# Bilinear products from twelve turned copies, and a full complex transform per image, in a four-layer kernel on one core

## The chip, the cores and the metric

The kernel runs on one core of a Trainium2 chip. The metric is the device time of one execution in microseconds (us). Three executions of the kernel before gave 5891.43, 5906.5 and 5907.27 us; their median is 5906.5. The first of them is the one that the profiler recorded.

## The reference

Four images of 96 channels and 64 x 64 pixels (4096 pixels each, also called tokens) pass through four layers: a recurrent (Mamba) layer with a fusion and a batch norm, a bilinear layer, and two token layers. Only the last three matter here. In the bilinear layer every pixel has a channel vector p (96 values, after a group norm and a 3 x 3 mean), and each output channel is a quadratic form in it. In a token layer the pixels are normed, widened to 192 channels, taken through a Fourier transform over all 4096 tokens, changed frequency by frequency, and brought back; a feed-forward pass with 8-bit rounding follows.

```python
# layer 1
wm = weight * mask
t = jnp.einsum('nlc,ocd->nlod', p, wm)
y = jnp.einsum('nlod,nld->nlo', t, p) + bias
...
# layers 2 and 3, attention
h = jax.nn.relu(_bn(jnp.einsum('bnc,hc->bnh', x, w1), ...))
X = jnp.fft.fft(h, axis=1, norm='ortho')
xr = jax.nn.relu(X.real * rd - X.imag * idg + rb)
xi = jax.nn.relu(X.imag * rd + X.real * idg + ib)
y = jnp.fft.ifft(xr + 1j * xi, axis=1, norm='ortho').real
o = _bn(jnp.einsum('bnh,ch->bnc', y, w2), ...)
...
# layers 2 and 3, feed-forward
h = jax.nn.relu(_qlinear(x, W1, b1))
y = _qlinear(h, W2, b2)
```

The mask of the bilinear weights has a zero diagonal and keeps about one entry in ten, but the kernel treats all pairs of channels alike. Since a quadratic form is symmetric, the weights of (c, d) and (d, c) can be added, and each unordered pair needs one product: 96 x 97 / 2 = 4656 of them.

## The kernel before

One function per stage runs after the other. `_mamba` (to about 2977 us) and `_norms_and_pool` (line 437) are the same in both kernels. The last thing that the norms do is to write the pooled image twice, one copy under the other, to a DRAM buffer `p2[b]` of 192 rows (line 523), so that any turn of the channels is one run of rows.

`_bilinear` (line 526) first makes the weights: seven groups of seven rotations are loaded on SP's queue into staging tiles with two buffers each (lines 535 to 551), masked and summed on VectorE into `wk`. Then it goes through 4 images and 4 column blocks of `CW` = 1024 pixels. For each block it loads the 96 channels `p0`, and for each of 48 turns k = 1 to 48 the channels turned by k (`rot`, 384 KB each, eight buffers, line 565); VectorE multiplies the two into `z` (line 566; k = 0 is a square on ScalarE, line 562), and TensorE adds weights times `z` to `p_y` by two matmuls of N = 512 columns with 96 rows (line 568). So there are 49 products a block. After four blocks the image is turned to token order by TensorE and written to DRAM as `tok[b]` on SP's queue (line 583).

`_tokens` (line 586) begins with loads and small calculations for the parameters of both layers (lines 598 to 649), then loads all four images as two tiles of an image pair (lines 840 to 845). For each layer it runs `attention` for pair 0 and pair 1 and then `ffn` for both; `finish` writes both pairs at the end. An attention works on two images together:

- `stats` takes mean and variance with one `bn_stats` per token row on VectorE (line 665); `normed` applies them on GpSimd, four rows at a time (line 683).
- Each group of four rows is transposed on TensorE (`plt`, line 699), copied by ScalarE (`lnT`), multiplied by `w1` (`ph`, line 706, N = 192) and clamped on VectorE into `dst`.
- The transform of 4096 = 128 x 32 is done in two steps. The first, `pa` (line 714), takes 32 matmuls of N = 384 (192 channels of two images) against tables `k_fwd` that hold 64 cosines and 64 sines, half of the frequencies, since the input is real. Three 128 x 4096 transposes on VectorE (line 722) bring the result to channel order, and `px` (line 730) does the second step with 96 matmuls of N = 128, whose stationary operand is a strided slice of the transposed tile.
- ScalarE and VectorE apply the change by frequency (lines 739 to 756), with the two special frequencies apart (`ends`); `pv` (lines 761 to 765) multiplies by `w2`, so that the way back has 96 channels instead of 192.
- `pg` (lines 777 to 779) and `poo` (line 787) are the two steps back. `poo` takes 32 matmuls of N = 192 for both images, and VectorE adds the result to the tokens.

`ffn` (line 791) is a chain by groups of four rows: norm, rounding to 8 bits, transpose, three matmuls `pf1` with a copy and a clamp each, rounding (`hq`, one buffer), twelve small matmuls `pf2`, copy, two adds.

Inside the recurrent stage the order is written by hand (`manual_schedule`). Elsewhere a scheduler of the framework orders the instructions of each engine's queue, by the dependences and the buffers free; within a queue the order is then fixed.

Of the kernel before, what the change touches and what calls it, by code (L numbers as in the profile page):

```python
# [9 lines left out]
F32 = mybir.dt.float32  # L10
# [17 lines left out]
H = 192  # L28
# [4 lines left out]
NROT = C // 2 + 1  # L33
CW = 1024

_V_LNG, _V_LNB = 0, 2
_V_GPB, _V_FUSB, _V_BNG, _V_BNB, _V_L1B = 4, 5, 6, 7, 8
_NV = 9
# [487 lines left out]
def _bilinear(ctx, tc, io, w, f_all, p2, tok):  # L526


    nc = tc.nc
    wp = ctx.enter_context(tc.tile_pool(name="bw", bufs=1))  # L530
    stage = ctx.enter_context(tc.tile_pool(name="bst", bufs=2))
# [5 lines left out]
    NK = 7  # L537
    wk = wp.tile([C, NROT, C], F32, name="wk", tag="wk")
    for k0 in range(0, NROT, NK):
        part = []  # L540
        for n, (lo, hi) in (("1", (0, NROT)), ("2", (1, NROT - 1))):
            a, e = max(k0, lo), min(k0 + NK, hi)
            wt = stage.tile([C, NK, C], F32, name=f"wt{n}_{k0}", tag=f"wt{n}")
            mt = stage.tile([C, NK, C], F32, name=f"mt{n}_{k0}", tag=f"mt{n}")
            nc.sync.dma_start(wt[:, : e - a, :], io["bw" + n][:, a - lo : e - lo, :])
            nc.sync.dma_start(mt[:, : e - a, :], io["bm" + n][:, a - lo : e - lo, :])
            out = wk[:, a:e, :] if n == "1" else wt[:, : e - a, :]
            nc.vector.tensor_tensor(out, wt[:, : e - a, :], mt[:, : e - a, :], ALU.mult)
            part.append((a, e, wt))
        a, e, wt = part[1]  # L550
        nc.vector.tensor_tensor(wk[:, a:e, :], wk[:, a:e, :], wt[:, : e - a, :], ALU.add)

    for b in range(B):
        for q in range(L // CW):
            cols = slice(q * CW, (q + 1) * CW)
            p0 = work.tile([C, CW], F32, name=f"p0_{b}_{q}", tag="p0", bufs=2)
            nc.sync.dma_start(p0, p2[b][0:C, cols])
            p_y = ps.tile([C, CW], F32, name=f"py2_{b}_{q}", tag="py2")
            for k in range(NROT):
                z = work.tile([C, CW], F32, name=f"z_{b}_{q}_{k}", tag="z")  # L560
                if k == 0:
                    nc.scalar.activation(z, p0, AF.Square)  # L562
                else:
                    rot = work.tile([C, CW], F32, name=f"rot_{b}_{q}_{k}", tag="rot", bufs=8)
                    nc.sync.dma_start(rot, p2[b][k : k + C, cols])
                    nc.vector.tensor_tensor(z, p0, rot, ALU.mult)  # L566
                for n in range(CW // 512):
                    nc.tensor.matmul(  # L568
                        p_y[:, n * 512 : (n + 1) * 512],
                        wk[:, k, :],  # L570
                        z[:, n * 512 : (n + 1) * 512],
                        start=(k == 0),
                        stop=(k == NROT - 1),
                    )
# [11 lines left out]
def _tokens(ctx, tc, io, w, tok, out):  # L586

    nc = tc.nc
    wp = ctx.enter_context(tc.tile_pool(name="tw", bufs=1))
    ps_x = ctx.enter_context(tc.tile_pool(name="tpsx", bufs=3, space=PSUM))
    ps = ctx.enter_context(tc.tile_pool(name="tps", bufs=5, space=PSUM))
    ident = w["ident"]
    H2 = 2 * H
# [3 lines left out]
    mats = _load(nc, wp, io["k_mats"].rearrange("p (a m) -> p a m", a=4), [128, 4, 128], "mats")  # L600
    bd, bd0, ibd, ibd0 = (mats[:, i, :] for i in range(4))
    att = _load(nc, wp, io["att"], [128, 2 * 12], "att")
    neg = wp.tile([128, 2 * 12], F32, name="neg", tag="neg")
    nc.vector.tensor_scalar(neg, att, -1.0, None, ALU.mult)  # L604

    prm = []
    with tc.tile_pool(name="tset", bufs=1) as sp:
        for i in range(2):
            d = {}
            bn1 = sp.tile([C + 1, 4, H], F32, name=f"bn1_{i}", tag="ld1")  # L610
# [12 lines left out]
            for h in range(4):  # L623
                nc.vector.tensor_tensor(d["w2"][:, h], d["w2"][:, h], s2, ALU.mult)
# [29 lines left out]
    def large(name, shape):  # L654
        n = 1
        for s in shape:
            n *= s
# [346 lines left out]
```

## Time and profile before

| | |
|---|---|
| median of three executions | 5906.5 us |
| the profiled execution: its own time | 5891.43 us |
| its span in the trace | 5889.6 us |
| granted TensorE clock, mean | 0.898 |
| TensorE busy | 4825.0 us (82%) |
| VectorE busy | 4617.2 us (78%) |
| ScalarE busy | 2609.6 us (44%) |
| GpSimd busy | 3007.2 us (51%) |
| recurrent stage | 0 to about 2977 us |
| norms and pooling | to about 3144 us |
| bilinear stage: weights, then products | 3144 to 3178, to 4538 us |
| token stage: parameters and first loads | 4538 to 4603 us |
| four attentions of two images | 4603 to 4838, to 5048; 5245 to 5450, to 5660 us |
| feed-forward passes, two images twice | 5048 to 5245; 5660 to 5853 us |
| `finish` | 5853 to 5889.6 us |

The span runs from the first instruction to the last; an execution's own time lies a little above it. In the page's rows, `PE` is TensorE and `PEld` its loading of stationary operands. The tokens stage's times come from the first and last instruction on the tiles named above. A matmul on fp32 data leaves two records in the trace, so 1568 bilinear matmuls appear as 3136 records. The mean of a group of records is the time that the trace gives one record, and neighbours overlap; how long a matmul holds the engine is read from the distance between starts.

### The profile page before, as it was taken

Reading aid. Unit: us, or ns where it says so; the run is one execution under the profiler, and the core shown is the slowest. Engines: PE = TensorE matmul, PEld = TensorE weight load, DVE = VectorE, ACT = ScalarE, POOL = GpSimd, SP = SyncE. Lnnn points to the kernel's source line nnn. Section 1 sums busy time; section 2 is a strip of 40 time slices with the busy share of each in tenths; the row PEclk is TensorE's granted clock in tenths of the full one; section 3 lists DMA queues with packets and bytes.
Section 4 is the critical chain, followed back from the end, with each engine's and each line's share of the span. In section 5 each row is a group of like instructions: output and inputs, shape, how many; then the busy total and the mean of one; then the engine's idle time right before and its main releaser. Section 6 shows DMA issues by size and latency. Waiting matters only on the chain.

```text
span 5889.6 us, 47897 instructions
## 1 busy us (share of the span) xinstructions
PE 4825.0 (82%) x13508; PEld 2140.2 (36%) x13508; DVE 4617.2 (78%) x5787; ACT 2609.6 (44%) x5545; POOL 3007.2 (51%) x2129
## 2 busy tenths in 40 slices
PE   7888888888888898888714999999998577567765
PEld 2333333333333333333201333333333466346643
DVE  5999999999999999999995767767675475756564
ACT  5676676666766766666520000000000155335445
POOL 5999999999999999999910000000000211230211
PEclk9999999999999999999956999999999688668875
DMA  4453543534535445344347888888886200000001
GB/s 103 93 119 72 111 104 79 121 85 98 116 71 117 94 88 119 80 103 107 76 134 202 234 233 232 230 235 229 235 230 179 73 15 15 15 3 20 22 11 43
DMA packets 167379, 669.02 MB, mean 114 GB/s; under 512 B 28356, under 2 KB 31366, under 8 KB 132168
## 3 DMA queue, kind: packets, MB, share of 16 engines
q1 hardware_dynamic: 167112, 665.96, 45.2%
q8 instruction: 107, 1.75, 0.1%
q14 instruction: 160, 1.31, 0.1%
HBM read 630.20 MB, written 35.65 MB: 113 GB/s over the span
## 4 chain that ended last, share of the span: by engine, by line
PE 34%; DVE 7%; DMA 3%; ACT 3%; issue 2%; POOL 1%; SPq 1%; ACTq 0%; DVEq 0%; POOLq 0%
PE py L568 23%; PE ph L706 2%; PE px L730 2%; PE pf L819 1%; PE pv L761 1%; DVE hq L815 1%; PE pa L714 1%; ACT y L812 1%; DVE a L722 1%; DVE r L813 1%; PE pf L810 1%; PE pg L779 1%; DMA k_inv<-in_k_inv 1%; DMA k_fwd<-in_k_fwd 1%; PE pv L764 1%
## 5 line engine op out<-in xcount | busy, mean ns | idle before, releaser
L367 POOL TENSOR_TENSOR dbx<-du,bq 128x1024 f32<-128x1024 f32 x768 | 1804.5, 2355 | 3.3 <-DMA bq<-rows 3.2
L388 PE MATMUL py<-hc,ident 128*128 128x512 f32 x3072 | 1601.6, 627 | 134.5 <-DVE hc L377 110.0
L568 PE MATMUL py<-z,wk 96*96 96x512 f32 x3136 | 1350.6, 593 | 68.9 <-DMA rot<-p 68.9
L566 DVE TENSOR_TENSOR z<-p,rot 96x1024 f32<-96x1024 f32 x768 | 935.6, 1221 | 395.2 <-PE py L568 393.5
L374 DVE TENSOR_TENSOR_SCAN da<-da,hst,dbx 128x512 f32<-128x512 f32 x864 | 1099.4, 1272 | 1.2 <-POOL dbx L367 1.2
L361 ACT ACTIVATE da<-delta,aneg 128x512 f32<-128x512 f32 x1536 | 1058.7, 690 | 91.4 <-DVE hs L374 71.4
L388 PEld LDWEIGHTS py<-hc,ident 128*128 128x128 f32 x3072 | 555.8, 195 | 1095.2 <-issue 531.4
L377 POOL TENSOR_TENSOR hc<-hs,cq 128x512 f32<-128x512 f32 x672 | 854.1, 1271 | 185.9 <-DVE hs L374 99.0
L701 POOL MEMSET lnT<- 1x512 f32 x64 | 33.2, 520 | 1628.2 <-DVE neg L604 1564.4
L374 DVE TENSOR_TENSOR_SCAN hs<-da,hst,dbx 128x512 f32<-128x512 f32 x672 | 856.1, 1274 | 9.0 <-ACT da L361 9.0
L568 PEld LDWEIGHTS py<-z,wk 96*96 96x96 f32 x3136 | 511.3, 163 | 898.5 <-issue 829.5
L377 DVE TENSOR_TENSOR hc<-da,cq 128x512 f32<-128x512 f32 x864 | 597.8, 692 | 81.0 <-DMA cq<-rows 4.4
L562 ACT ACTIVATE z<-p 96x1024 f32<-96x1024 f32 x16 | 16.9, 1056 | 1292.5 <-PE py L568 1225.1
L381 ACT COPY hst<-da 128x1 f32<-128x1 f32 x864 | 136.3, 158 | 728.6 <-DVE hc L377 718.4
L683 POOL TENSOR_SCALAR x_f<-t,m_f,r_f 128x96 f32<-128x96 f32 x256 | 130.8, 524 | 512.6 <-DVE q L799 512.4
L224 PE MATMUL pc<-xs,taps 128*128 128x512 f32 x768 | 381.6, 594 | 0.0
L683 POOL TENSOR_SCALAR x_a<-t,m_a,r_a 128x96 f32<-128x96 f32 x256 | 107.8, 437 | 415.9 <-PE plt L699 352.0
L730 PE MATMUL px<-mats,a 128*128 128x128 f32 x768 | 184.2, 398 | 72.3 <-DVE a L722 69.9
L198 PE MATMUL pr<-r,picks 128*96 128x512 f32 x128 | 110.6, 965 | 151.6 <-DVE r L194 151.6
L224 PEld LDWEIGHTS pc<-xs,taps 128*128 128x128 f32 x768 | 145.7, 190 | 185.5 <-issue 175.3
L208 PE MATMUL pxz<-hn,in_w 96*64 96x512 f32 x768 | 212.0, 622 | 0.0
L730 PEld LDWEIGHTS px<-mats,a 128*128 128x128 f32 x768 | 174.1, 312 | 78.1 <-DVE a L722 74.7
(231 smaller groups left out, 5217.0 us busy)
## 6 DMA issues: line engine op xcount, KB each, us to landing
rot<-p SPq DMA_DIRECT2D x768, 384.0 KB, 4.3
bq<-rows SPq DMA_DIRECT2D x256, 512.0 KB, 6.8
cq<-rows SPq DMA_DIRECT2D x256, 512.0 KB, 10.2
p<-pt SPq DMA_DIRECT2D x8, 1536.0 KB, 12.6
k_fwd<-in_k_fwd SPq DMA_DIRECT2D x32, 256.0 KB, 2.8
k_inv<-in_k_inv SPq DMA_DIRECT2D x32, 256.0 KB, 2.7
x<-in_x SPq DMA_DIRECT2D x16, 384.0 KB, 9.1
fd<-f SPq DMA_DIRECT2D x32, 192.0 KB, 2.0
```

What stands on the lines that cost most here:

```text
L208: nc.tensor.matmul(q[h, :], in_w[:, l, 64 * kk : 64 * kk + 64], hn[b], start=True, stop=True)
L224: nc.tensor.matmul(p_c[k], taps[:, (l * 3 + k) * 4 + j, :], xs[k][:, j : j + TC], start=(j == 0), stop=(j == 3))
L361: nc.scalar.activation(da[u], st[n]["delta"][k], AF.Exp, scale=aneg[:, at : at + 1])
L367: nc.gpsimd.tensor_tensor(t, st[n]["du"][k].unsqueeze(1).to_broadcast([128, 2, TC]), b, ALU.mult)
L374: nc.vector.tensor_tensor_scan(hs[u], da[u], dbx[u], hst[:, at : at + 1], ALU.mult, ALU.add)
L377: (nc.gpsimd if on_pool(u) else nc.vector).tensor_tensor(hc[u], hs[u], c, ALU.mult)
L381: nc.scalar.copy(hst[:, at : at + 1], hs[u][:, TC - 1 : TC])
L388: nc.tensor.matmul(py[n, k], ident, hc.pop(u), start=(s == 0), stop=(s == 15))
L566: nc.vector.tensor_tensor(z, p0, rot, ALU.mult)
L568: nc.tensor.matmul(p_y[:, n * 512 : (n + 1) * 512], wk[:, k, :], z[:, n * 512 : (n + 1) * 512], start=(k == 0), stop=(k == NROT - 1),)
L683: nc.gpsimd.tensor_scalar(x[:, j, :], t[:, k, :], m[:, k : k + 1], r[:, k : k + 1], ALU.add, ALU.mult)
L730: nc.tensor.matmul(p_x[:, k, :], a2[:, 128 * m : 128 * m + 128, k0 + k], bd0 if k0 + k == 0 else bd, start=True, stop=True,)
```

## The change

In the bilinear stage the 49 products a block of 96 rows become 37. Twelve turned tiles of 128 rows (96 rows turned by one shift, and the first 32 rows of another shift below them, two DMAs each from `p2`) are loaded once a block, each kind with two buffers. The products are one square (96 rows, ScalarE) and 36 products of one of the first six tiles with one of the last six (128 rows, VectorE). The shifts are chosen so that each pair of channels occurs; where a pair occurs twice, the second weight is zero. The weights are correspondingly 128 x 37 x 96, loaded in ten groups of four products, with one staging buffer of each kind. Matmuls keep N = 512. In SP's new order, the loads of turned tiles 0 to 5 of the first block stand between the weight groups, those of tiles 6 to 11 after all of them; the store of `tok[b]` stands after the first turned loads of the next image, and the token stage's first loads (image 0, first parameters) stand ahead of the last such store.

In the token layers the transform of half of the frequencies for a pair of images becomes a full complex transform for one image at a time, so there are eight attentions instead of four:

- `layernorm` works on a whole image: two reductions, a subtraction and a multiplication of 128 x 3072 on VectorE and a square on ScalarE, in place of `stats` and `normed`; GpSimd has only the small fills left.
- `k_fwd` and `k_inv` hold all 128 cosines and 128 sines (512 KB a table of four rows, three buffers). `pa` becomes 64 matmuls of N = 192, the transposes four of 128 x 3072, `px` 128 matmuls of N = 256 with 96 channels of stationary operand, two accumulated into one result.
- The change by frequency is two ScalarE instructions (`cross`) and two VectorE instructions (`zz`) for each of 16 tiles, without special frequencies.
- `pv` becomes 128 matmuls of N = 96 with two copies for each pair of k, `pg` 24 of N = 512 in pairs, and `poo` for each of 32 rows one matmul with a single row (the shift of the second norm) and two with the tables, N = 96 each.
- Images are taken in pairs, one pair after the other: load two, both layers, `finish`, then the next two. The large tiles share four `slot` buffers of 24 KB a partition; `px` has two PSUM buffers of two banks and all else four.

`ffn` keeps its steps, on a whole-image norm, with two buffers for `hq` and a tile of its own (`o2`) for the first add. Constants and layouts change to match (`_layout`, `_constants`). The diff's core, with removed lines that the listing above shows left out:

```diff
-NROT = C // 2 + 1
 CW = 1024
...
+_TURNS = [(s, (32 * (i % 3) + 16 * (i // 3)) % C) for i, s in enumerate((0, 76, 60, 44, 32, 88))]
+_TURNS += [(s, 32 * (i % 3) + (2, 6)[i // 3]) for i, s in enumerate((25, 1, 73, 49, 24, 48))]
+_PAIRS = [(0, 0)] + [(i, j) for j in range(6, 12) for i in range(6)]
...
     wp = ctx.enter_context(tc.tile_pool(name="bw", bufs=1))
-    stage = ctx.enter_context(tc.tile_pool(name="bst", bufs=2))
+    stage = ctx.enter_context(tc.tile_pool(name="bst", bufs=1))
+    turned = ctx.enter_context(tc.tile_pool(name="bturn", bufs=2))
     work = ctx.enter_context(tc.tile_pool(name="bwork", bufs=3))
     ps = ctx.enter_context(tc.tile_pool(name="bps", bufs=2, space=PSUM))
...
+    NK = 4
+    NT = len(_PAIRS)
+    wk = wp.tile([128, NT, C], F32, name="wk", tag="wk")
+    for k0 in range(0, NT, NK):
+        e = min(k0 + NK, NT)
         part = []
...
+        for n in "12":
+            wt = stage.tile([128, NK, C], F32, name=f"wt{n}_{k0}", tag=f"wt{n}")
+            mt = stage.tile([128, NK, C], F32, name=f"mt{n}_{k0}", tag=f"mt{n}")
+            nc.sync.dma_start(wt[:, : e - k0, :], io["bw" + n][:, k0:e, :])
+            nc.sync.dma_start(mt[:, : e - k0, :], io["bm" + n][:, k0:e, :])
+            out = wk[:, k0:e, :] if n == "1" else wt[:, : e - k0, :]
+            nc.vector.tensor_tensor(out, wt[:, : e - k0, :], mt[:, : e - k0, :], ALU.mult)
+            part.append(wt)
+        nc.vector.tensor_tensor(wk[:, k0:e, :], wk[:, k0:e, :], part[1][:, : e - k0, :], ALU.add)
     for b in range(B):
         for q in range(L // CW):
             cols = slice(q * CW, (q + 1) * CW)
-            p0 = work.tile([C, CW], F32, name=f"p0_{b}_{q}", tag="p0", bufs=2)
-            nc.sync.dma_start(p0, p2[b][0:C, cols])
+            rows = []
+            for i, (hi, lo) in enumerate(_TURNS):
+                t = turned.tile([128, CW], F32, name=f"turn{i}_{b}_{q}", tag=f"turn{i}")
+                nc.sync.dma_start(t[0:C, :], p2[b][hi : hi + C, cols])
+                nc.sync.dma_start(t[C:128, :], p2[b][lo : lo + 128 - C, cols])
+                rows.append(t)
             p_y = ps.tile([C, CW], F32, name=f"py2_{b}_{q}", tag="py2")
...
+            for k, (i, j) in enumerate(_PAIRS):
+                z = work.tile([128, CW], F32, name=f"z_{b}_{q}_{k}", tag="z")
+                m = C if i == j else 128
+                if i == j:
+                    nc.scalar.activation(z[:m], rows[i][:m], AF.Square)
                 else:
-                    rot = work.tile([C, CW], F32, name=f"rot_{b}_{q}_{k}", tag="rot", bufs=8)
-                    nc.sync.dma_start(rot, p2[b][k : k + C, cols])
-                    nc.vector.tensor_tensor(z, p0, rot, ALU.mult)
+                    nc.vector.tensor_tensor(z, rows[i], rows[j], ALU.mult)
                 for n in range(CW // 512):
...
+                    ns = slice(n * 512, (n + 1) * 512)
+                    nc.tensor.matmul(p_y[:, ns], wk[:m, k, :], z[:m, ns], start=(k == 0), stop=(k == NT - 1))
             nc.vector.scalar_tensor_tensor(f_all[b][:, cols], p_y, bias, f_all[b][:, cols], ALU.add, ALU.add)
...
+    slots = ctx.enter_context(tc.tile_pool(name="tslot", bufs=4))
+    work = ctx.enter_context(tc.tile_pool(name="twork", bufs=2))
+    ps_x = ctx.enter_context(tc.tile_pool(name="tpsx", bufs=2, space=PSUM))
+    ps = ctx.enter_context(tc.tile_pool(name="tps", bufs=4, space=PSUM))
...
+    def slot(name, dtype=F32):
+        return slots.tile([128, SLOT if dtype == F32 else 2 * SLOT], dtype, name=name, tag="slot")
+    def layernorm(u, t, out_dtype):
+        s = slot(f"ln_{u}")
+        xc = s[:, 0 : NJ * C].rearrange("p (j c) -> p j c", j=NJ)
+        sq = s[:, NJ * C :].rearrange("p (j c) -> p j c", j=NJ)
+        m = work.tile([128, NJ], F32, name=f"m_{u}", tag="m")
...
+        nc.vector.tensor_reduce(m, t, AX.X, ALU.add)
+        nc.vector.tensor_scalar(m, m, 1.0 / C, None, ALU.mult)
+        nc.vector.tensor_tensor(xc, t, m.unsqueeze(2).to_broadcast([128, NJ, C]), ALU.subtract)
+        nc.scalar.activation(sq, xc, AF.Square)
...
+        nc.vector.tensor_reduce(v, sq, AX.X, ALU.add)
+        nc.vector.tensor_scalar(v, v, 1.0 / C, None, ALU.mult)
+        r = _rsqrt(nc, work, v, [128, NJ], f"ln_{u}").unsqueeze(2).to_broadcast([128, NJ, C])
+        if out_dtype == F32:
+            nc.vector.tensor_tensor(xc, xc, r, ALU.mult)
+            return xc
+        q = work.tile([128, NJ, C], out_dtype, name=f"lnq_{u}", tag="lnq", bufs=1)
+        nc.vector.tensor_tensor(q, xc, r, ALU.mult, saturate=False)
+        return q
     def table(u, name, j0):
-        t = work.tile([128, 4, 128], F32, name=f"{name}_{u}_{j0}", tag="tab")
+        t = work.tile([128, 4, 256], F32, name=f"{name}_{u}_{j0}", tag="tab", bufs=3)
         nc.sync.dma_start(t, io[name][:, j0 : j0 + 4, :])
         return t
...
+        ln = layernorm(f"a{u}", t, F32)
...
+        a1 = [slot(f"a1{n}_{u}").rearrange("p (j h) -> p j h", j=NJ) for n in "ri"]
         for j0 in range(0, NJ, 4):
             tab = table(u, "k_fwd", j0)
...
+            for j in range(0, 4, 2):
+                for n in range(2):
+                    p_a = ps.tile([128, 2, H], F32, name=f"pa_{u}_{j0}_{j}_{n}", tag="ps")
+                    for jj in range(2):
+                        nc.tensor.matmul(
+                            p_a[:, jj, :],
+                            tab[:, j + jj, n * 128 : (n + 1) * 128],
+                            dst[:, j0 + j + jj, :],
+                            start=True,
+                            stop=True,
+                        )
+                    nc.scalar.copy(a1[n][:, j0 + j : j0 + j + 2, :], p_a)
+        a2 = []
+        for n in range(2):
+            s = slot(f"a2{n}_{u}").rearrange("p (h k) -> p h k", k=32)
+            for h in range(2):
+                hs = slice(h * C, (h + 1) * C)
+                nc.vector.transpose(s[:, hs, :], a1[n][:, :, hs].rearrange("p j h -> p h j"))
+            a2.append(s)
+        vs = slot(f"v_{u}").rearrange("p (n c k) -> p n c k", n=2, k=32)
+        for k0 in range(0, 32, 4):
+            zs = []
+            for h in range(2):
+                p_x = ps_x.tile([C, 4, 2, 128], F32, name=f"px_{u}_{k0}_{h}", tag="px")
+                for k in range(4):
+                    for n in range(2):
+                        nc.tensor.matmul(
+                            p_x[:, k].rearrange("p a m -> p (a m)"),
+                            a2[n][:, h * C : (h + 1) * C, k0 + k],
+                            bd[:, n, :],
+                            start=(n == 0),
+                            stop=(n == 1),
+                        )
+                x = work.tile([C, 4, 2, 128], F32, name=f"cross_{u}_{k0}_{h}", tag="cross")
+                nc.scalar.activation(x[:, :, 0, :], p_x[:, :, 1, :], AF.Identity, bias=d["rb"][h], scale=d["nid"][h])
+                nc.scalar.activation(x[:, :, 1, :], p_x[:, :, 0, :], AF.Identity, bias=d["ib"][h], scale=d["id"][h])
+                z = work.tile([C, 4, 2, 128], F32, name=f"zz_{u}_{k0}_{h}", tag="zz", bufs=4)
+                nc.vector.scalar_tensor_tensor(
+                    z.rearrange("p k a m -> p (k a m)"),
+                    p_x.rearrange("p k a m -> p (k a m)"),
+                    d["rd"][h],
+                    x.rearrange("p k a m -> p (k a m)"),
+                    ALU.mult,
+                    ALU.add,
                 )
...
+                nc.vector.tensor_scalar(z, z, 0.0, None, ALU.max)
+                zs.append(z)
+            for k in range(0, 4, 2):
+                p_v = ps.tile([128, 2, 2, C], F32, name=f"pv_{u}_{k0}_{k}", tag="ps")
+                for kk in range(2):
+                    for n in range(2):
+                        for h in range(2):
+                            nc.tensor.matmul(
+                                p_v[:, kk, n, :], zs[h][:, k + kk, n, :], d["w2"][:, h, :], start=(h == 0), stop=(h == 1)
+                            )
+                for n in range(2):
+                    o = vs[:, n, :, k0 + k : k0 + k + 2].rearrange("p c k -> p k c")
+                    nc.scalar.copy(o, p_v[:, :, n, :])
+        gs = slot(f"g_{u}").rearrange("p (n j c) -> p n j c", n=2, c=C)
+        for c0 in range(0, C, 16):
+            for n in range(2):
+                p_g = ps.tile([128, 16, 32], F32, name=f"pg_{u}_{c0}_{n}", tag="ps")
+                for m in range(2):
                     nc.tensor.matmul(
+                        p_g.rearrange("p c k -> p (c k)"),
+                        ibd[:, (0, 2, 1, 0)[2 * n + m], :],
+                        vs[:, m, c0 : c0 + 16, :].rearrange("p c k -> p (c k)"),
+                        start=(m == 0),
+                        stop=(m == 1),
                     )
...
+                nc.vector.transpose(gs[:, n, :, c0 : c0 + 16].rearrange("p j c -> p c j"), p_g)
         for j0 in range(0, NJ, 4):
             tab = table(u, "k_inv", j0)
...
+            p_o = ps.tile([128, 4, C], F32, name=f"poo_{u}_{j0}", tag="ps")
+            for j in range(4):
+                nc.tensor.matmul(p_o[:, j, :], one, d["sh2"], start=True, stop=False)
+                for n in range(2):
+                    nc.tensor.matmul(
+                        p_o[:, j, :], tab[:, j, n * 128 : (n + 1) * 128], gs[:, n, j0 + j, :], start=False, stop=(n == 1)
+                    )
+            nc.vector.tensor_tensor(t[:, j0 : j0 + 4, :], p_o, t[:, j0 : j0 + 4, :], ALU.add)
...
+    def ffn(u, d, t):
+        q = layernorm(f"f{u}", t, F8)
+        q16 = slot(f"q16_{u}", BF16)[:, 0 : NJ * C].rearrange("p (j c) -> p j c", j=NJ)
+        nc.scalar.copy(q16, q)
...
+    for b0 in range(0, B, 2):
+        pair = range(b0, min(b0 + 2, B))
+        for b in pair:
+            ts[b] = work.tile([128, NJ, C], F32, name=f"t_{b}", tag="t")
+            nc.sync.dma_start(ts[b], tok[b])
+        for i in range(2):
+            for b in pair:
+                attention(f"{b}_{i}", prm[i], ts[b])
+            for b in pair:
+                ffn(f"{b}_{i}", prm[i], ts[b])
+        for b in pair:
+            finish(b)
```

## The prediction

> **What bounds the kernel now.** I read the stage windows first, then the costliest groups and the waits inside the stages that the diff touches, then the TensorE timeline for the pace of one matmul. The recurrent stage (to about 2977 us) and the norms are the same code in both kernels; what changes begins at 3144 us. The windows (columns: busy us of PE, PEld, DVE, ACT, POOL with instruction counts, granted clock, DMA share, GB/s) are, in order, the bilinear stage, the start of the token stage, an attention of two images, and the four feed-forward passes:
>
> ```profile
> 3180.00:4538.00 1358.00, 1356.99 (x3230) 521.65 (x3229) 953.15 (x783) 26.99 (x39) 0.00 (x0) 1.00 0.83 230
> 4538.00:4603.00 65.00, 5.11 (x32) 4.24 (x32) 20.93 (x99) 4.97 (x12) 0.99 (x2) 0.53 0.44 154
> 4838.00:5048.00 210.00, 158.80 (x744) 133.63 (x743) 124.28 (x253) 96.26 (x194) 41.47 (x96) 0.86 0.07 20
> 5048.00:5245.00 197.00, 99.58 (x628) 55.03 (x626) 141.42 (x481) 83.09 (x163) 57.24 (x112) 0.51 0.01 4
> ```
>
> The reader is to see two limits. In the bilinear stage TensorE is busy for all of 1358 us at full clock: it is the bound. The waits of that stretch say the same, since VectorE waits for TensorE to free its products and almost never for a transfer:
>
> ```profile
> DVE z L566 <- PE py L568: 393.5, 724, 2.2
> ...
> DVE z L566 <- DMA rot<-p: 1.8, 2, 1.5
> ```
>
> In the attention TensorE is busy for 159 of 210 us, and the rest are hand-offs. Its parts, in order: first transform (pa), the DVE transposes (a), second transform with w2 (px, pv), inverse (pg), last inverse (poo):
>
> ```profile
> 4679.60:4703.00 23.40, 22.42 (x65) 12.02 (x64) 0.56 (x1) 14.85 (x31) 0.52 (x1) 0.96 0.28 79
> 4703.00:4727.50 24.50, 6.45 (x25) 5.49 (x25) 23.87 (x9) 6.18 (x14) 0.00 (x0) 0.55 0.04 11
> 4727.50:4806.00 78.50, 68.09 (x356) 66.92 (x357) 48.88 (x92) 63.01 (x128) 0.00 (x0) 0.89 0.00 1
> 4806.00:4822.00 16.00, 14.50 (x54) 8.63 (x53) 10.63 (x12) 1.62 (x2) 0.00 (x0) 0.95 0.00 0
> 4822.00:4838.00 16.00, 11.28 (x60) 9.68 (x61) 13.58 (x51) 0.00 (x0) 0.00 (x0) 1.00 0.32 99
> ```
>
> Only in the transposes does TensorE stand still (24.5 us, clock 0.55). Its pace comes from the timeline; one fp32 matmul leaves two records:
>
> ```profile
> 5274.70 0.60 PE L699 MATMUL plt<-ident,x_a 128*96 128x128 f32 x4
> 5276.07 1.54 PE L706 MATMUL ph<-w,lnT 97*128 97x192 f32 x8 [0.77 <-POOL x_a L683]
> 5277.45 0.60 PE L699 MATMUL plt<-ident,x_a 128*96 128x128 f32 x4
> ...
> 4743.74 0.61 PE L765 MATMUL pv<-w,sd 128*128 128x96 f32 x4
> 4744.19 0.52 PE L761 MATMUL pv<-w,sd 128*128 128x192 f32 x2
> ```
>
> Four matmuls of N=192 start within 1.38 us (0.34 each); the pv of N=96 start 0.195 to 0.22 apart in the same timeline. The bilinear stage gives N=512: 1360 us over 1568 matmuls, 0.867 each. That is 1.67 ns per column plus about 0.02 us, so N=256 is put at 0.44 us. The strided weights of px are a second limit for it: in the timeline its N=128 matmuls start 0.445 apart already, two weight loads of 0.22 us each, where columns alone would take 0.23; at N=256 the two limits tie.
>
> **What the Trainium skill says.** "FP8 and Floating Point Precision", TensorE Precision Notes: true FP32 takes four passes through the array. The trace agrees in sum: 4 x 512 columns at the 2.4 GHz of the next page are 0.853 us, and 0.867 is measured. So fp32 columns are what counts, and the number of rows (96 or 128) is free. "TensorE: Matmul & The Clock Gate", What's actually happening: the clock halves after an idle window of about 3.4 us and returns after a busy one. The trace agrees on halving (0.55 in the transposes), but the return is slower: 0.84 over the 16.5 us after them. "VectorE: DVE Perf Modes", The perf-mode tier table: fp32 tensor_tensor runs at 1x, tensor_scalar at 2x from SBUF. The trace agrees: 96x1024 products 1.221 us, 96x4096 tensor_scalar 2.409 us (0.59 ns per element).
>
> **The change, bilinear part.** 49 products a block become 37, in 16 blocks, two matmuls each: 16 x 12 x 2 x 0.867 = -333 us. Cover: VectorE makes 36 products at 1.22 us (same elements per partition), 44 us a block against 64 us of TensorE. Loads fall from 49 to twelve 512 KB tiles a block, 6.3 MB, about 27 us at the measured 230 GB/s, one block ahead in a second buffer: hidden, and if not they would cost at most those 27 us a block. In the new SP order the token store is issued after the next image's first loads, so it holds nothing up.
> The start gets worse. Weights now use single staging buffers in ten groups, and the tiles for the second product (turn 6) are queued behind all of them on SP. Before, weights ran from 3144 to 3177 us at 249 GB/s, 7.1 MB. Now 7.3 MB plus about 3.6 MB of turned tiles must land, 44 us at that rate, and each group waits for its multiply: about 53 us. I take +20; bounds 0 (weights still hidden by bandwidth) and +45 (every group a full 7 us round trip).
>
> **The change, token part.** The diff also replaces the half-frequency transform of two images at once by a full complex one, image by image. Eight attentions instead of four, each alone with as many or more columns. TensorE per image, from the paces above:
> - plt and ph: eight groups at the 2.75 us of the timeline, 22.
> - pa: 64 x 0.34 = 21.9 (before: 23.4 for two images).
> - transposes: four of 128x3072 at 7.09 x 3/4 = 5.3; px needs the third before its sums can close, so TensorE stands 16.6.
> - px: 128 of N=256 x 0.44 = 56; pv: 128 of N=96 x 0.195 = 25; restart at half clock over 16 us of work, +8; joints 2: 91. ScalarE (32 x 0.57 and 32 copies near 0.47: 33) and VectorE (16 x (1.28 + 0.66) = 31) lie beneath.
> - last chain to pg: 4.7. pg: 24 x 0.867 = 20.8, but the new layer norm of the next step (three passes of 128x3072 at 3.3 us) stands between its twelve 1.03 us transposes on VectorE's queue, and poo needs all of them: 26.6.
> - poo: 96 of N=96 x 0.195 = 18.7, with its 512 KB tables at the edge, 19.5 (upper bound: 2.7 us a table, 22).
> The sum is 202 us an image; 8 x 202 = 1616, plus 24 for four starts from the cold clock of the feed-forward: 1640. Before: 235 + 210 + 205 + 210 = 860. So +780.
> GpSimd's normalisation (437 to 524 ns each) goes, but 2.75 us was already a period without waiting long for it. Feed-forward: per group the same chain of matmul, copy, r, hq, pf2; whole-image norm replaces bn_stats. 49.5 us an image against 48.8, +6; bounds -70 (VectorE's busy time of about 40 us an image) and +50 (the norm is not hidden). The token start: 65 us become about 55, since image 0's load is queued before the last block's end: -10 (bounds -20, +10). Pairs now run one after the other: the second pair's load (8 us) and norm (19 us) follow the first pair's output transposes, 37 us in the middle and 26 at the end against 36.6: +26.
> Sum: 20 - 333 - 10 + 780 + 6 + 26 = +489. The profiled execution has a span of 5889.6 and a time of 5891.4 us; 5891.4 + 489 = 6380. That execution lies 15 us under the median of 5906.5, so 6395.
>
> **Rivals.**
> *Cold clock.* The attention's TensorE runs at the 0.86 granted in three of the four attentions now. Its 156 us of work become 181, 17 more than the 8 counted: 8 x 17 = +139, 6535. For it: the new gaps (16.6 us a transform, a slow pg). Against: the dense part leaves no gaps, and the bilinear stage held 1.00.
> *Overlap.* The norms slip past pg and transposes hide under other matmuls: about 178 us an image, 8 x -24, 6205. Against: in the new order TensorE's px follows pa of the same image at once.
> *TensorE is not the token bound.* If its columns were hidden, VectorE's 93 us an image would set the pace: 8 x 93 = 744, total about 5500, faster. It decides below 140 us an image (6395 falls to 5906 when 8 x 61 go). But TensorE's own 156 us at full clock already exceed 140.
> *Name only:* that the bilinear gain fails is excluded, as 384 matmuls go from a stage with no TensorE idle.
>
> **Numbers.** Forecast 0.66, cold clock 0.16, overlap 0.14, hidden columns 0.04. A difference within 0.3% is about what a measurement of this kernel can't tell from none. Range: it ends at the two neighbouring cases, 6205 and 6535 (rounded to 6540), so that about half of each and the hidden columns lie outside, 0.07 + 0.08 + 0.04 = 0.19; the bounds of start, feed-forward and tables lie inside. Faster 0.03, same 0.01, slower 0.96.
>
> **What would show it.** Right: about 1184 bilinear matmuls at the same pace over 1027 us; px, pv, pa and pg at the top of the groups; attentions of about 200 us, eight of them; transposes the only long TensorE idle. Wrong: VectorE as releaser in px, a bilinear stage that waits for turned tiles, N=256 pace above 0.5 us (strided weights), or attentions under 180 us.

## The result and the profile after

The changed kernel takes 6739.31 us (median of four executions, 6720.06 to 6752.21) where the kernel before takes 5898.97 on the same chip (four executions). The ratio is 1.1424, 95% interval 1.1385 to 1.1464. The sign was forecast; the time lies 199 us above the upper end of the range. The profiled executions (6750.4 us of span against 5889.6) differ by 861 us, and the stages account for all of it. The boundaries below are first matmuls of a tile in the trace's timeline and the edges of the windows shown (the products of the changed kernel are counted from the second one, at 3198 us; the square alone ran at 3155). Both columns are differences to the kernel before, rounded to whole us.

| stage | predicted | measured |
|---|---|---|
| recurrent stage, norms | 0 | +2 |
| start of the bilinear products | +20 | +18 |
| bilinear products | -333 | -333 |
| start of the token stage | -10 | +10 |
| attentions (eight against four pairs) | +780 | +1081 |
| feed-forward | +6 | +65 |
| middle and end | +26 | +17 |
| sum | +489 | +861 |

The stage windows of the profile after, in the same columns as before (length, then busy us and counts of PE, PEld, DVE, ACT and POOL, granted clock, DMA share, GB/s): the loading of the weights, the products, the start of the token stage, and the feed-forward of two images in the first and in the second token layer:

```profile
3155.00:3197.00 42.00, 3.73 (x4) 0.95 (x4) 13.88 (x28) 0.01 (x1) 0.00 (x0) 0.50 0.82 233
3198.00:4225.00 1027.00, 1026.80 (x2460) 396.55 (x2460) 719.91 (x591) 26.97 (x39) 0.00 (x0) 1.00 0.38 99
4225.00:4301.00 76.00, 5.92 (x35) 4.55 (x34) 36.23 (x75) 7.69 (x14) 1.18 (x3) 0.53 0.35 118
4783.10:4901.00 117.90, 48.46 (x305) 26.27 (x305) 79.55 (x135) 41.76 (x68) 0.00 (x0) 0.50 0.02 5
5385.00:5490.00 105.00, 48.50 (x305) 26.31 (x305) 65.75 (x123) 38.96 (x66) 0.00 (x0) 0.50 0.02 5
```

TensorE is still busy for all of the bilinear products at clock 1.00, for 1027 us where the prediction said 1027. The first attention, part by part (plt and ph; pa; transposes; px and pv; pg; then poo in three pieces):

```profile
4300.80:4337.40 36.60, 30.04 (x97) 25.91 (x98) 9.04 (x19) 4.65 (x8) 3.64 (x7) 0.50 0.00 0
4337.40:4359.10 21.70, 21.70 (x129) 21.41 (x127) 0.65 (x2) 14.83 (x31) 0.52 (x1) 0.96 0.56 164
4359.10:4364.40 5.30, 0.01 (x1) 0.00 (x0) 5.30 (x2) 0.48 (x1) 0.00 (x0) 0.85 0.39 125
4364.40:4468.00 103.60, 92.24 (x512) 87.79 (x512) 47.28 (x35) 35.42 (x62) 0.00 (x0) 0.90 0.00 1
4468.50:4491.10 22.60, 22.57 (x49) 9.71 (x49) 18.32 (x19) 3.30 (x3) 0.00 (x0) 0.92 0.00 0
4491.10:4500.00 8.90, 6.81 (x31) 5.35 (x30) 3.79 (x4) 0.00 (x0) 0.00 (x0) 0.77 0.00 0
4500.00:4520.00 20.00, 20.00 (x71) 16.24 (x70) 2.23 (x4) 0.00 (x0) 0.00 (x0) 0.50 0.27 79
4520.00:4547.40 27.40, 27.40 (x95) 22.27 (x95) 1.67 (x3) 0.00 (x0) 0.00 (x0) 0.50 0.26 77
```

The last two lines are the surprise. TensorE is busy for 20.00 of 20.00 us and waits for nothing, yet its clock is 0.50. Poo takes 56.4 us here (55.9 in the mean of the eight) where 19.5 were expected. The TensorE timeline shows one row of poo as a one-row matmul (`1*128`, the shift) and two with 128 rows:

```profile
4494.68 0.46 PE L782 MATMUL poo<-sh,one 1*128 1x96 f32 x2
4495.07 0.69 PE L784 MATMUL poo<-g,k_inv 128*128 128x96 f32 x4
4495.69 0.53 PE L782 MATMUL poo<-sh,one 1*128 1x96 f32 x2
4496.14 1.17 PE L784 MATMUL poo<-g,k_inv 128*128 128x96 f32 x4
4497.24 0.74 PE L782 MATMUL poo<-sh,one 1*128 1x96 f32 x2
4497.91 1.17 PE L784 MATMUL poo<-g,k_inv 128*128 128x96 f32 x4
4499.01 0.74 PE L782 MATMUL poo<-sh,one 1*128 1x96 f32 x2
```

From one row to the next are 1.01 us at first (4494.68 to 4495.69) and 1.77 later (4497.24 to 4499.01): the clock fell in between. Records of the same row count start 0.112 us apart, but around each change of the row count two starts in succession are 0.19 to 0.21 us apart: 0.17 us more for each change (1.01 us a row instead of 6 x 0.112). The expectations below call the 0.187 us start the pause. So there were two suspects, the few rows and the pauses.

### The profile page after: what moved, and what is told of

It is laid out like the page before. It is cut to its first block, busy times and chain, and to the rows that moved or that the text cites. A ratio compares the mean times of both kernels' runs of the same rounds, so it can differ in the third digit from the quotient of the medians.

```text
span 6750.4 us, 53489 instructions
## 1 busy us (share of the span) xinstructions
PE 5577.3 (83%) x17540; PEld 2945.7 (44%) x17540; DVE 4665.3 (69%) x4925; ACT 2713.6 (40%) x5577; POOL 2767.0 (41%) x1618
## 4 chain that ended last, share of the span: by engine, by line
PE 40%; DVE 10%; ACT 3%; issue 2%; DMA 2%; SPq 0%; ACTq 0%; POOL 0%; DVEq 0%; POOLq 0%
PE py L581 15%; PE px L731 7%; PE poo L784 4%; PE pv L757 4%; PE ph L697 2%; PE pa L707 2%; PE poo L782 2%; DVE a L721 1%; ACT y L804 1%; PE pf L811 1%; DVE g L776 1%; DVE hq L807 1%; PE plt L690 1%; PE pf L802 0%; DMA bn<-in_bn 0%
## 5 line engine op out<-in xcount | busy, mean ns | idle before, releaser
L581 PE MATMUL py<-z,wk 128*96 128x512 f32 (+1 forms) x2368 | 1022.6, 594 | 83.6 <-DMA mt<-in_bm 44.2
L578 DVE TENSOR_TENSOR z<-turn,turn 128x1024 f32<-128x1024 f32 x576 | 703.0, 1224 | 302.2 <-PE py L581 280.4
L581 PEld LDWEIGHTS py<-z,wk 128*96 128x96 f32 (+1 forms) x2368 | 386.3, 164 | 710.2 <-issue 624.1
L731 PE MATMUL px<-bd,a 128*96 128x256 f32 x2048 | 505.4, 401 | 107.6 <-DVE a L721 107.6
L731 PEld LDWEIGHTS px<-bd,a 128*96 128x96 f32 x2048 | 444.9, 245 | 137.8 <-DVE a L721 122.5
L742 DVE SCALAR_TENSOR_TENSOR zz<-px,vec,cross 96x1024 f32<-96x1024 f32 x128 | 163.8, 1280 | 396.8 <-ACT cross L740 396.8
L787 DVE TENSOR_TENSOR t<-poo,t 128x384 f32<-128x384 f32 x64 | 35.7, 557 | 388.9 <-PE poo L784 388.9
L739 ACT ACTIVATE cross<-px,vec,nid 96x512 f32<-96x512 f32 x128 | 99.0, 774 | 478.2 <-PE px L731 478.2
L757 PE MATMUL pv<-w,zz 96*128 96x96 f32 x2048 | 269.3, 289 | 25.2 <-DVE zz L750 25.2
L784 PE MATMUL poo<-g,k_inv 128*128 128x96 f32 x1024 | 287.4, 435 | 3.2 <-DVE g L776 3.2
## 6 DMA issues: line engine op xcount, KB each, us to landing
p<-pt SPq DMA_DIRECT2D x8, 1536.0 KB, 12.6
```

The costliest lines, as they stand in the source:

```text
L578: nc.vector.tensor_tensor(z, rows[i], rows[j], ALU.mult)
L581: nc.tensor.matmul(p_y[:, ns], wk[:m, k, :], z[:m, ns], start=(k == 0), stop=(k == NT - 1))
L731: nc.tensor.matmul(p_x[:, k].rearrange("p a m -> p (a m)"), a2[n][:, h * C : (h + 1) * C, k0 + k], bd[:, n, :], start=(n == 0), stop=(n == 1),
L742: nc.vector.scalar_tensor_tensor(z.rearrange("p k a m -> p (k a m)"), p_x.rearrange("p k a m -> p (k a m)"), d["rd"][h], x.rearrange("p k ...
L757: nc.tensor.matmul(p_v[:, kk, n, :], zs[h][:, k + kk, n, :], d["w2"][:, h, :], start=(h == 0), stop=(h == 1))
L784: nc.tensor.matmul(p_o[:, j, :], tab[:, j, n * 128 : (n + 1) * 128], gs[:, n, j0 + j, :], start=False, stop=(n == 1))
```

## The experiments

### The one-row matmuls

**Without them.** The shift goes to the zero frequency of v, as in the kernel before:

```diff
+        dc = vs[0:1, 0, :, 0]
+        nc.vector.tensor_tensor(dc, dc, d["sh2"], ALU.add)
...
-                nc.tensor.matmul(p_o[:, j, :], one, d["sh2"], start=True, stop=False)
```

> The changed kernel without the one-row matmuls of poo; the shift is added to the zero frequency of v before pg, as the kernel before does it. Theory A (matmuls with one active row count as idle for the clock, so poo halves its own clock): poo falls from 56 us an image to 64 matmuls at 0.224 us, about 15, at clock 1.0, and the next plt and ph start warmer; about 370 us less than the changed kernel, some 6370 us. Theory B (narrow matmuls of N = 96, or the short wait between pg and poo, halve the clock whatever the rows): poo keeps clock 0.5 and takes 64 x 0.43 = 28 us; about 230 us less, some 6510 us.

Measured: 6414.43 us, 325 less; ratio to before 1.0895 (1.0855 to 1.0936).

**With 128 rows, zeros in 127 of them.** Same matmuls in the same order:

```diff
-    one = wp.tile([1, 128], F32, name="one", tag="one")
-    nc.gpsimd.memset(one, 1.0)
+    one = wp.tile([128, 128], F32, name="one", tag="one")
+    nc.gpsimd.memset(one, 0.0)
+    nc.gpsimd.memset(one[0:1], 1.0)
...
-        d["sh2"] = wp.tile([1, C], F32, name=f"sh2_{i}", tag=f"sh2_{i}")
+        d["sh2"] = wp.tile([128, C], F32, name=f"sh2_{i}", tag=f"sh2_{i}")
+        nc.gpsimd.memset(d["sh2"], 0.0)
```

> The changed kernel with the same 96 matmuls of N = 96 in poo, but the shift operands are filled with zeros to 128 rows. Theory A (rows active set the clock): poo at clock 1.0, 96 x 0.224 = 22 us an image instead of 56, about 275 us less than the changed kernel in all, 6465. Theory B (narrow matmuls or the wait before poo): clock 0.5 stays, 96 x 0.43 = 41 us, about 120 us less, 6620.

Measured: 6434.7 us, 305 less; ratio 1.0934 (1.0884 to 1.0984). Poo takes 23 to 26 us, 24.1 in the mean. The windows of poo in these two kernels, first without and then with filled rows:

```profile
4490.00:4507.00 17.00, 15.13 (x126) 14.46 (x127) 5.04 (x9) 0.00 (x0) 0.00 (x0) 1.00 0.62 196
```

```profile
4484.00:4505.00 21.00, 20.59 (x184) 20.43 (x184) 5.41 (x9) 0.00 (x0) 0.00 (x0) 1.00 0.53 158
```

Clock 1.00 in both. The second kernel differs from the changed one in nothing but the number of rows of these matmuls (and of their stationary operand), so narrow matmuls of N = 96 and the seam before poo are out as the cause; nor does it matter that 127 of the rows hold zeros. In the first, a part of the 17 us instead of the expected 15 are the inverse tables: the timeline has two waits of 0.47 us for `k_inv` between 4490 and 4500 us.

**The other way round: one-row matmuls in the kernel before.**

```diff
-                    nc.tensor.matmul(p_o[:, jj, :], tab[:, j + jj, :], gs[:, j0 + j + jj, :], start=True, stop=True)
+                    nc.tensor.matmul(p_o[:, jj, :], one, d["sh2"].rearrange("p b c -> p (b c)"), start=True, stop=False)
+                    nc.tensor.matmul(p_o[:, jj, :], tab[:, j + jj, :], gs[:, j0 + j + jj, :], start=False, stop=True)
```

> The kernel before with a one-row matmul of N = 192 ahead of each of poo's 32 matmuls, in place of the addition to the zero frequency. Theory A: poo, 16 to 18 us at clock 1.0 now, halves its clock and takes 45 to 50 us in each of the four attentions, about 120 us more in all, 6020. Theory B (the clock is set by narrow matmuls or by the seam before poo, not by rows): clock stays at 1.0 with N = 192, poo takes about 27 us, 40 us more in all, 5940.

Measured: 6074.9 us, 190 more than before; ratio 1.0327 (1.0287 to 1.0368). Poo goes from 16.4 to 56 us in each of the four attentions, at clock 0.52 with TensorE busy throughout, and one of the following plt and ph grew from 51 to 72 us. The size was underestimated, the direction holds: the mechanism isn't bound to the new transform.

**Rows or pauses?** Fill 32 or 64 rows; merge the one-row matmuls of four or two rows of poo into one; use one row in all of poo.

> As the run with the shift operands filled to 128 rows, but to 32 rows only. If the mean of the active rows decides (here (128 + 128 + 32) / 3 = 96 rows, as many as pv has at full clock), or any number of rows clearly above one: poo about 24 us an image at clock 1.0 and a total near 6435. If every matmul with few rows counts as idle: poo stays near 45 to 56 us at clock 0.5 and the total is 6600 to 6740.

Measured: 6743.16 us, poo 55 to 56 us. 32 rows behave as one.

> The shift operands filled with zeros to 64 rows. After 32 rows behaved as one row (6743 us) and 128 rows did not (6435): if a matmul has to fill more than half of the rows to count as work, 6740 again with the pause at each change of the row count; if 64 rows are enough, about 6435 with poo near 24 us at clock 1.0. If the pause goes at 64 rows and the clock stays low, rows and not pauses set the clock (poo about 41 us, 6600).

Measured: 6728.97 us, poo 55 to 57 us, TensorE busy throughout at half clock, and the pause is still there. With 128 rows it is gone (0.112 throughout).

```profile
4482.00:4530.00 48.00, 48.00 (x166) 38.94 (x167) 3.90 (x7) 0.00 (x0) 0.00 (x0) 0.50 0.25 77
```

The edit of the run that merges the one-row matmuls of four rows:

```diff
+            nc.tensor.matmul(p_o.rearrange("p j c -> p (j c)"), one, d["sh2x4"], start=True, stop=False)
...
-                nc.tensor.matmul(p_o[:, j, :], one, d["sh2"], start=True, stop=False)
```

> The changed kernel with one one-row matmul of N = 384 for four rows of poo in place of four of N = 96: the same columns with one active row (384 of 1152 in each group), but two changes between one row and 128 rows in place of eight. Theory A (time with few active rows counts as idle): the share is the same, poo stays at clock 0.5 with about (2 x 0.64 + 16 x 0.214 + 0.2) x 8 = 39 us an image; total about 6600. Theory C (the pauses at each change of the row count, 0.187 us from start to start where 0.112 is the pace, are what counts as idle): clock 1.0, poo about (0.64 + 16 x 0.112 + 0.15) x 8 = 21 us, total about 6440.

Measured: 6453.3 us, poo 24 to 26 us, at clock 1.00 but for one stretch of 3.4 us at its start in seven of the eight attentions. The same columns with one row, spread over fewer changes, leave the clock up:

```profile
4494.52 0.91 PE L784 MATMUL poo<-sh2x,one 1*128 1x384 f32 x2
4495.36 2.02 PE L787 MATMUL poo<-g,k_inv 128*128 128x96 f32 x16
4497.31 0.91 PE L784 MATMUL poo<-sh2x,one 1*128 1x384 f32 x2
4498.15 2.02 PE L787 MATMUL poo<-g,k_inv 128*128 128x96 f32 x16
```

That spoke for the pauses, and against theory A in its plain form. The next run speaks against the pauses alone. Starting from the kernel of the first experiment, poo multiplies one row only:

```diff
-                        p_o[:, j, :], tab[:, j, n * 128 : (n + 1) * 128], gs[:, n, j0 + j, :], start=(n == 0), stop=(n == 1)
+                        p_o[:, j, :], tab[0:1, j, n * 128 : (n + 1) * 128], gs[0:1, n, j0 + j, :], start=(n == 0), stop=(n == 1)
```

> The kernel of the first experiment (shift at the zero frequency, 64 matmuls of N = 96 in poo, 17 us at clock 1.0), where poo multiplies only the first of its 128 rows; it leaves the rest of the last inverse step out. All matmuls have one active row and no change of the row count lies between them. If few rows count as idle in any way: clock 0.5 in poo and at least 28 us. If only the changes of the row count do it: clock 1.0 and the same 17 us, 6414 in all.

Measured in a single execution: 6501.49 us, poo 25 to 27 us. In this window its clock is 0.50, with no change of the row count and no wait:

```profile
4490.00:4507.00 17.00, 17.00 (x81) 17.00 (x81) 2.79 (x5) 0.00 (x0) 0.00 (x0) 0.50 0.55 164
```

So few rows alone do halve the clock.

> As the run with one one-row matmul for four rows of poo, but one of N = 192 for two rows: the share of one-row columns is a third again, and there are four changes of the row count in four rows of poo, between the two (clock 1.0, 26 us) and the eight (clock 0.5, 56 us). If there is a threshold on the share of the pauses and it lies above 13%: clock 1.0, about 27 us, total 6460. If below: clock 0.5, about 48 us, 6640.

Measured in a single execution: 6661.43 us, poo 44 to 46 us, at half clock but for its start:

```profile
4500.00:4530.00 30.00, 30.00 (x108) 23.91 (x107) 3.21 (x6) 0.00 (x0) 0.00 (x0) 0.50 0.33 102
```

> As the run with one one-row matmul of N = 384 for four rows of poo (26 us an image, clock 1.0), but with two of them, each adding half of the shift. The changes of the row count stay two in four rows; the time in which columns stream through 128 active rows falls from 1.28 of 2.80 us (46%) to 1.28 of about 3.65 us (35%). The runs so far halved the clock at 0% (one row only), 39% (1, 32 and 64 rows) and 43% (by twos), and kept it at 46% and more. If that share decides: clock 0.5 in poo, about 45 us an image, total near 6600. If the number of changes of the row count decides: clock 1.0, about 33 us, total near 6500.

Measured: 6608.44 us; ratio 1.1208 (1.1091 to 1.1325). Poo took 51 or 52 us in five attentions, 46 in one, and 29 at full clock in the other two. The shares in this expectation were reckoned from the pace of single records. By the distance from row to row at full clock, columns stream through 128 rows for 32% of the time in the changed kernel (0.32 of 1.01 us, with the prediction's 1.67 ns a column), 37% in two by fours (1.28 of 3.44), 46% by fours (1.28 of 2.79) and 47% by twos (0.64 of 1.36). Yet the run by twos fell to half clock in every attention, so this share alone doesn't order the runs.

**A count that does order them.** In all kept traces the granted clock is either 1.00 or 0.50, and it changes only at multiples of 3.41 us. For each such stretch inside an attention, add up the time that TensorE's records need for their columns at full clock (0.83 ns a column for each fp32 record, half of a matmul's 1.67), each weighted by its rows out of 128, and divide by 3.41 us. A limit of 0.364 on this share was fitted on the six kernels whose attentions have no matmuls with few rows; it misses the clock of the next stretch in 31 of their 2191 stretches. In the eight other kernels it misses 44 of 4050, and 9 of 777 in poo. Without the weight by rows, and with its own fitted limit, the count misses 218 and 77; a guess that the clock stays as it is misses 388 and 66. The count was made after the runs, and none was made to test it.

It fits the mixed cases. In the changed kernel's poo the weighted share is 0.19 to 0.29 in the stretches at full clock, so the clock falls, and 0.17 to 0.24 at half clock, so it stays down; with filled rows it is mostly 0.71 and more. A stretch at half clock gets fewer columns done (pa has a share of 0.50 there, against 0.98 at full clock), so the same work can hold the full clock and yet not win it back. By fours, the one stretch at half clock reaches 0.37, and the clock returns; by twos, poo falls at its start, where the timeline has waits for `g`, and then reaches 0.36 at most. Two by fours have mostly 0.35 to 0.38 at full clock, at the limit itself.

### The bilinear half alone

The token layers of the kernel before, with the new `_bilinear` and its constants.

> The kernel before with the new bilinear stage alone (half-frequency token layers of the kernel before). By the windows of the two profiles, which give the new stage 20 us more until the products run and 333 less in them, and if the halves are independent: 313 us less than before, about 5586 us. If the new stage owes its gain to the new token stage's earlier loads or spoils the old one's start, the token stage's start of 65 us grows by 10 to 25 and the time is 5595 to 5610.

Measured: 5560.51 us against 5884.72 on its chip, 324 less; ratio 0.9448 (0.9412 to 0.9484). The halves are independent, within 11 us. The start of the token stage didn't suffer: from the last product to pa are 124 us, where the kernel before has 143.

**The start of the products.** The first block's turned tiles 0 to 6 ahead of the weights, tiles 7 to 11 between them:

```diff
+    first = {i: turn(i, 0, 0) for i in (0, 6, 1, 2, 3, 4, 5)}
...
+        i = 6 + k0 // (2 * NK) + 1
+        if (k0 // NK) % 2 == 0 and i < 12:
+            first[i] = turn(i, 0, 0)
```

> The new bilinear stage in the kernel before (5560 us), with the first block's turned tiles 0 to 6 loaded ahead of the weights and tiles 7 to 11 between the weight groups. If the later start (20 us) is the wait for all weights and then tile 6: the products start after 3.6 MB and one weight group, about 20 us after the last store of the pooled image instead of 53, and 25 to 33 us go, about 5530. If weights and tiles are needed at the rate at which they arrive anyway, or each weight group waits for the multiply of the one before (single staging buffers): the products start earlier but then stall, and at most 10 us go.

Measured: 5535.14 us against 5882.17; ratio 0.9399 (0.9356 to 0.9441), the fastest kernel of the study, about 25 us below the one without early turns. The windows from 3160 to 3180 us, with late and with early turns:

```profile
3160.00:3180.00 20.00, 0.00 (x0) 0.00 (x0) 7.26 (x13) 0.00 (x0) 0.00 (x0) 0.50 0.78 232
```

```profile
3160.00:3180.00 20.00, 14.82 (x30) 5.62 (x31) 12.77 (x17) 0.00 (x0) 0.00 (x0) 0.77 0.81 230
```

The transfers run at the same rate; only their order lets TensorE begin. The first image's products end at 3424 us instead of 3450.

### The norm in the feed-forward

The first experiment's kernel, with `stats` and `normed` of the kernel before in `ffn` only:

```diff
-        q = layernorm(f"f{u}", t, F8)
+        m, rr = stats(f"f{u}", t)
         for j0 in range(0, NJ, 4):
+            x = normed(f"f{u}", t, j0, m, rr)
```

> The changed kernel with the shift added to the zero frequency (as in the first experiment, 6414 us), and in the feed-forward the row-wise norm of the kernel before (bn_stats on VectorE, the normalisation on GpSimd, rounding by groups of four rows) in place of the whole-image norm. If the 3.35 us passes of the whole-image norm stand in VectorE's queue between the links of the feed-forward's chain: each pass of two images falls from 118 and 105 us to about 98, 4 passes, 55 us less, some 6360. If the passes grew for another reason (TensorE's clock, PSUM with four buffers instead of five, single images): no change, 6400 to 6420, or slower by GpSimd's 0.53 us rows.

Measured: 6373.64 us, 41 less; ratio 1.0828 (1.0794 to 1.0862). The four passes take 104, 93, 105 and 93 us, together 49 less than the first experiment's 445; some of it came back in plt and ph (235 us over eight instead of 223). VectorE's timeline of the changed kernel shows what lay in the way:

```profile
4788.14 3.36 DVE L665 TENSOR_TENSOR ln_f<-t,m_f 128x3072 f32<-128x3072 f32 x1
4791.41 0.35 DVE L805 TENSOR_SCALAR r<-y,fb 128x512 f16<-128x512 f16 x1
4791.79 0.96 DVE L807 CAST hq<-r 128x1536 fp8e5<-128x1536 f16 x1
4794.32 3.35 DVE L668 TENSOR_REDUCE v_f<-ln_f 128x32 f32<-128x3072 f32 x1 [1.57 <-ACT ln_f L666]
4797.60 0.35 DVE L817 TENSOR_TENSOR o<-o,fb 128x384 f16<-128x384 f16 x1
4797.86 0.41 DVE L798 COPY qT<-pqt 96x512 bf16<-96x512 bf16 x1
...
4801.16 3.35 DVE L675 TENSOR_TENSOR lnq_f<-ln_f,ln_f_r 128x3072 fp8e5<-128x3072 f32 x1
4804.43 0.95 DVE L807 CAST hq<-r 128x1536 fp8e5<-128x1536 f16 x1
```

`r`, `hq` and `qT` are the chain's links, and each stands here behind a pass of about 3.35 us of the next image's norm. The second layer's passes are the shorter ones (105 us): no further norm follows them inside a pair.

## Why the prediction was wrong

**Right.** The bilinear products (-333), the later start with its cause (the queue order; 18 of the predicted 20 us), the sign, and the bound: the attention's TensorE work. Transposes, px and pv together measured 108.9 us an image (5.3 and 103.6) against 107.6. TensorE's wait of 16.6 us came apart, 5.3 us ahead of px and the rest inside it, since px may start on the first transpose. pv's pace was 0.224 us, where the prediction took the lower end of its 0.195 to 0.22: 3.7 us an image.

**Wrong: the step "poo: 96 of N=96 x 0.195 = 18.7".** It rested on "So fp32 columns are what counts, and the number of rows (96 or 128) is free". The trace of before showed that for 96 and 128; the step used it for one row. Poo took 55.9 us an image, 36.4 too many: 8 x 36.4 = 291. The eight attentions took 1949 us where 1640 were forecast, 309 too many (the four before took 868, not the 860 of the prediction); plt and ph add 72 and pg takes 64 off again, so the rest nearly cancels by luck. Of the 36.4, about 13 are pauses and pace (1.01 x 32 = 32.3 at full clock, against 19.5), the remaining 24 the halved clock. The first two experiments show that the one-row matmuls are the cause: they give back 325 and 305 us, and their times of 6414 and 6435 lie inside the range forecast.

**Wrong in its reach: plt and ph at 22 us.** They took 34.0, because 2.75 us a group holds at full clock, and after poo the clock was down. Without the one-row matmuls they take 28 in the mean; what remains over the 22 + 3 are the starts after a feed-forward pass or a pause (26.7 to 36.7 us, against 22.4 right after poo). In the count of the experiments plt and ph of the changed kernel have shares of 0.41 to 0.55 at full clock and 0.26 to 0.39 (median 0.29) at half clock, so they mostly keep the clock that they start with.

**Too high: the norm on pg.** pg and the chain ahead of it took 23.3 us, not 31.3. A pass of the norm does run there (VectorE is busy for 18.32 us in that window, twelve transposes of 1.05 us being 12.6), but TensorE hardly waits for it. Where the norm cost time was the feed-forward: "the norm is not hidden" was the +50 bound of that step, and +65 was measured, 49 of which the row-wise norm takes back.

**The token start** took 75 us instead of 55. The chain of waits has two loads of the parameters `bn` in it, which the earlier load of image 0 doesn't shorten:

```profile
4225.56 15.40 DMA bn<-in_bn
...
4271.85 14.52 DMA bn<-in_bn
```

VectorE has the variance of image 0 at 4268 us, but takes the next step of this norm only 27 us later. In its queue the calculations for the second layer's parameters stand between, and these wait for the second `bn`. No experiment was made on it.

```profile
4268.01 0.17 DVE L669 TENSOR_SCALAR v_a<-v_a 128x32 f32<-128x32 f32 x1
...
4286.40 0.26 DVE L432 TENSOR_SCALAR s_ve<-bn 97x192 f32<-97x192 f32 x1 [11.93 <-DMA bn<-in_bn]
...
4294.86 0.17 DVE L432 TENSOR_SCALAR ln_a_ve<-v_a 128x32 f32<-128x32 f32 x1
```

**The rivals.** *Cold clock* named the right quantity for the wrong reason (gaps), and so priced it at 139 us. "Against: the dense part leaves no gaps" was no argument: the clock fell where TensorE had none. The Trainium skill, "TensorE: Matmul & The Clock Gate", What's actually happening, ties the clock to how busy the array has been; here an array that shows busy for 20.00 of 20.00 us was granted 0.50, and the runs differ by the rows of their matmuls. The busy column doesn't tell what the clock follows; columns weighted by rows tell it in all but 9 of 777 stretches of poo. *Overlap* and *hidden columns* are out: px, pv and poo hold TensorE as forecast or longer.

## What to carry to other kernels

A stage's new operation must be priced with its own shape, the row count of a matmul included: one with a single row among full ones was here neither free nor merely one more, and adding a constant elsewhere, or filling its operands with zeros, gave back over 300 us. When a change joins two edits, take them apart before judging it: the bilinear half alone is 5.5% faster than the kernel before, though the whole is 14% slower. Long passes on an engine that also carries a chain of short links can delay each link: here a link stood behind a pass of 3.35 us, and taking the passes out gave back 49 us in four feed-forward passes.

## What the runs showed of the hardware

TensorE's granted clock fell to 0.50 during uninterrupted work when matmuls had one row (alone, or between full ones), and with 32 and 64 rows between full ones. With 128 rows, zeros in 127 of them, it was 1.00 in seven of eight poos and 0.93 in the other. In px and pv, with 96 rows in pv, it was 0.90 with the wait at their start.

The clock of a stretch of 3.41 us follows the work of the stretch before, counted in columns weighted by rows: full above a share of about 0.36, half below, in all but 75 of 6241 stretches of the attentions of fourteen kernels. Why the limit lies there stays open.

A change of the row count between matmuls costs about 0.17 us (1.01 us for a row of six records, where 0.112 each make 0.67), with 1, 32 and 64 rows alike.
